# Attention and quantized feed-forward on one core: the gate's tokens prepared a step sooner, a piece per chunk, an earlier fetch, and idle products at the change of stages

## The chip, the core and the metric

The kernel runs on one core of a Trainium2 chip. A core has a matrix engine (TensorE, PE in the profile, with its weight loads in a row PEld of its own), a vector engine (VectorE, DVE), a scalar engine (ScalarE, ACT), a general engine (GpSimd, POOL) and a queue that issues transfers (SyncE, SP). Each engine takes its instructions in the order of the program. The metric is the device time of one execution in microseconds; of several executions the median is given.

## What is computed

The input `x` has 16 elements of 512 tokens of width 512. A cross attention with 16 heads over 120 context rows is added to it, then a feed-forward with gate and up weights (1536 x 512) and a down weight (512 x 1536). Both take a layer-normalized input:

```python
x = x + _L0_xattn_ref(_layernorm(x, axis=-1), ctx_1024, ctx_1024, Wq, Wk, Wv, Wo)
x = x + _L0_ffn_ref(_layernorm(x, axis=-1), w_gate, w_up, w_down)

def _L0_ffn_ref(x, w_gate, w_up, w_down):
    x = act_qdq(x)
    up = act_qdq(x @ lpbq_dequant(w_up).T)
    gate = act_qdq(x @ lpbq_dequant(w_gate).T)
    sig = fixed_qdq_u16(jax.nn.sigmoid(gate))
    gate = act_qdq(gate * sig)
    o = act_qdq(gate * up)
    return o @ lpbq_dequant(w_down).T
```

`act_qdq` rounds a whole tensor to 16-bit integers by a scale that comes from its largest absolute value. The scale of the feed-forward's input is therefore known only when the attention of all 16 elements is done, the gate's only when all gate products are done, and so on. That makes stages: attention, gate, up, down. `lpbq_dequant` rounds a weight to 4 bits in blocks of 32.

## The kernel before

**Attention** (lines up to 670) works through the 16 elements, transposes and quantizes the gate's weights on the way and leaves each element's output in `x1_d` in DRAM, with the mean and inverse deviation of each row in `ln_mv` and `ln_rstd`. Its last element ends with four output products (`output`, L416), row statistics, and a maximum of the normalized rows (`largest`). The first element of the feed-forward is held back transposed in the tiles `first`.

**The gate stage** (from line 674) first takes the largest value over all partitions (`over_all`: a product `line_x` at L694 and one `every_x` at L700) and from it the scale. Tokens are held as 16-bit integers (`xq`, one buffer). [...]each block of 128 features of an element is split into three *pieces*: the high part `hi` (`split_high`, L743), the low part `lo` (`split_low`, L746) and a mix `mix` of both (`split_mix`, L753). There are four blocks per element, and 8 buffers of each piece, that is two elements.

The work of an element is six chunks of two blocks of 128 gate outputs: 16 x 6 = 96 chunks, in order. `step(i)` is written so that TensorE runs ahead by half a chunk: `begin(i+1)` puts 8 products of the mixes into a new PSUM tile (L832; three tiles), ACT copies chunk i-1 out (L850, `t`, three buffers), `divide(i+1)` scales the new tile on ACT (L838), a `middle()` follows, then `rest(i)` adds 16 products of low and high pieces (L767), then an `after()`. In what follows, *step f of element b* is `step(6 b + f)`. `begin` of the first chunk of element b+1 stands at the head of step 5 of element b and is the first to read the pieces of b+1.

The preparation of element b+1 is spread over these hooks, by hand:

- `load` (L879, SP): `x1_d[b+2]` into the one buffer `x1t`, after step 2 of element b
- `normalize` (L883, POOL): four operations, after step 4
- `quantize` (L891, ACT, and L894, SP): a cast of the tile to 16-bit integers and a transposing transfer into `xq`, in the middle of step 0 of the next element (step 1 for element 1)
- `high`: four operations on POOL after steps 1 and 2 (for element 1: two on VectorE and two on POOL, after steps 3 and 4)
- `low` with the mix: two blocks after step 2, one after step 3, one after step 4 (for element 1: two after step 3, two after step 4)
- `keep` (L804, SP) stores `xq` for the up stage after step 2; `short_mixes` (L810, ACT) shortens the mixes and stores them too.

After each step VectorE also takes two maxima of chunk i-1 (`largest`, L855), and the dictionary `jobs` holds the preparation of the up weights (12 blocks, one per element from element 1 on) and of the down weights (4 blocks of three times the size, turned in elements 3, 6, 9, 12): load, quantize on VectorE (L142 to L152), turn on TensorE (L160), and the rest on VectorE, ACT and POOL (L169 to L172) with stores on SP. `when` gives the steps of the four jobs of an up weight.

The order on TensorE, VectorE, ACT and POOL in the gate stage is that of the program text (`manual_schedule`); SP's order is found by the compiler. The weights come through `Weights.load` (L738): 36 tiles of 256 KB on SP, 12 before the tokens of element 0, 24 after `load(1)`.

Of the kernel before, what the change touches and what calls it, by code (L numbers as in the profile page):

```python
# [9 lines left out]
F32 = mybir.dt.float32  # L10
# [11 lines left out]
P = 128  # L22
# [31 lines left out]
def tile_xattn_ffn(  # L54
# [32 lines left out]
    ident = const.tile([P, P], F32, name="ident")  # L87
# [12 lines left out]
    x1_d = [dram.tile([NQ, P, D], F32, name=f"x1_{b}") for b in range(B)]  # L100
# [22 lines left out]
    class WeightBlock:  # L123
# [7 lines left out]
        def load(self):  # L131
            self.wt = self.pool.tile(
                [P, self.I], F32, tag=f"raw_{self.tag}", name=f"wt_{self.nm}", bufs=1
            )
            nc.sync.dma_start(self.wt, self.w[ts(self.o, P), :])

        def quantize(self):
            pool, I, tag, nm = self.pool, self.I, self.tag, self.nm
            nb = I // WBLOCK
            wb = self.wt.rearrange("p (n k) -> p n k", k=WBLOCK)  # L140
            s = pool.tile([P, nb], F32, tag=f"s_{tag}", name=f"ws_{nm}", bufs=1)
            nc.vector.tensor_reduce(s, wb, AX.X, ALU.max, apply_absolute_value=True)  # L142
            nc.vector.tensor_scalar(s, s, 1.0 / 7.0, SCALE_MIN, ALU.mult, ALU.max)
            r = pool.tile([P, nb], F32, tag=f"r_{tag}", name=f"wr_{nm}", bufs=1)
            nc.vector.reciprocal(r, s)
            q = pool.tile([P, I], I16, tag=f"q_{tag}", name=f"wq_{nm}", bufs=1)
            qb = q.rearrange("p (n k) -> p n k", k=WBLOCK)
            nc.vector.tensor_tensor(
                qb, wb, r.unsqueeze(2).to_broadcast([P, nb, WBLOCK]), ALU.mult
            )  # L150
            nc.vector.tensor_scalar(q, q, 7.0, -8.0, ALU.min, ALU.max)
            nc.vector.tensor_tensor(  # L152
                wb, qb, s.unsqueeze(2).to_broadcast([P, nb, WBLOCK]), ALU.mult
            )
# [28 lines left out]
    with ExitStack() as at:  # L183
# [12 lines left out]
        def bank(nm):  # L196
            return ps_w.tile([P, 512], F32, tag="w", name=nm)
# [78 lines left out]
        class Element:  # L276
# [195 lines left out]
        ones = wpool.tile([P, P], F32R, name="ones")  # L472
# [34 lines left out]
        rep = wpool.tile([P, NG, P], F32R, name="rep")  # L507
# [161 lines left out]
        last.end_normalize(NQ - 1, nc.vector)  # L669
        last.largest(NQ - 1)  # L670

    H = S // 2
    N2 = NF // 2
    small = ctx.enter_context(tc.tile_pool(name="small", bufs=1))
# [6 lines left out]
    ones = small.tile([2, P], F32, name="ones")  # L681
# [91 lines left out]
    flat = lambda t: t.rearrange("p h f t -> p (h f t)")  # L773
    halves = lambda t: t.rearrange("p f (h t) -> p h f t", t=H)
    part = lambda t, b, f: t[b, :, :, 2 * f : 2 * f + 2, :]
# [5 lines left out]
    with ExitStack() as gu:  # L781
# [5 lines left out]
        class Tokens:  # L787


            def __init__(self, b, nm):  # L790
                self.b, self.nm, self.p = b, f"{nm}_{b}", []
                self.q = xpool.tile([P, NQ, ND, P], I16, tag="xq", name=f"xq_{self.nm}", bufs=1)

            def high(self, d, engine):
# [17 lines left out]
                    nc.sync.dma_start(xn_d[self.b], self.n)  # L812

            def fetch(self):
                nc.sync.dma_start(self.q, xq_d[self.b])
                self.n = xpool.tile([P, ND, S], I16, tag="xn", name=f"xn_{self.nm}", bufs=1)
                nc.sync.dma_start(self.n, xn_d[self.b])
# [4 lines left out]
        class Chunk:  # L822
# [25 lines left out]
            def out(self, dst):  # L848
                self.t = xpool.tile([P, 2, 2, H], F32, tag="t", name=f"t_{self.nm}", bufs=3)
                nc.scalar.copy(self.t, halves(self.ps))  # L850
# [8 lines left out]
        wp = wprep.__enter__()  # L859
        wg = Weights(wg_d, "wg")  # L860
        wu = Weights(wu_d, "wu")
        wd = Weights(wd_d, "wd")
        wg.load((0, 1), (0,))
        wg.load((0, 1), (1, 2))
        wg.load((2, 3))
        s_x, r_x = scale_of(over_all([max_x], "x"), 1.0, "x")
        s_xw = small.tile([P, 1], F32, name="s_xw")

        xs = {0: Tokens(0, "g")}
        for i, t in enumerate(first):  # L870
            nc.vector.tensor_scalar(
                xs[0].q[:, 2 * i : 2 * i + 2], t.rearrange("p q (d t) -> p q d t", t=P),
                r_x, None, ALU.mult,
            )

        def load(b):
            xs[b] = Tokens(b, "g")
            xs[b].x1 = wp.tile([P, NQ, D], F32, tag="x1t", name=f"x1t_{b}", bufs=1)
            nc.sync.dma_start(xs[b].x1, x1_d[b].rearrange("q p d -> p q d"))  # L879

        def normalize(b):
            for q in range(NQ):
                nc.gpsimd.tensor_scalar(  # L883
                    xs[b].x1[:, q, :], xs[b].x1[:, q, :],
                    ln_mv[:, b, q, 0:1], ln_rstd[:, b, q : q + 1], ALU.subtract, ALU.mult,
                )

        def quantize(b):

            xi = wp.tile([P, NQ * D], I16, tag="xi", name=f"xi_{b}")  # L890
            nc.scalar.activation(  # L891
                xi, xs[b].x1.rearrange("p q d -> p (q d)"), AF.Copy, scale=r_x
            )
            nc.sync.dma_start_transpose(xs[b].q.rearrange("p q d t -> p (q d) t"), xi)  # L894


# [22 lines left out]
        for d in range(ND):  # L919
            xs[0].high(d, nc.vector if d < 2 else nc.gpsimd)  # L920
            xs[0].low(d)
        xs[0].keep()
        load(1)
        normalize(1)
        wg.load(range(4, NF))
        nc.vector.tensor_scalar(s_xw, s_x, WHOLE, None, ALU.mult)

# [10 lines left out]
        def step(i, before=None, middle=None, after=None):  # L938
# [14 lines left out]
            if after:  # L953
                after()

        chunks[0].x = xs[0]
        chunks[0].begin()
        chunks[0].divide()
# [2 lines left out]
        jobs = {}  # L961
        for o in range(NF):
            start = (o + 1) * N2
            when = ((1, 2, 4, 5), (0, 1, 3, 4), (0, 1, 4, 5))[o % 3]
            for j, job in zip(when, up_weight(o)):
                jobs.setdefault(start + j, []).append(job)
        for o in range(ND):
            start = (3 * o + 2) * N2
            for j, job in zip((4, 5, 7, 8, 9, 10), down_weight(o)):
                jobs.setdefault(start + j, []).insert(0, job)  # L970
        for b in range(B):
            for f in range(N2):
                i = b * N2 + f

                def middle():
                    if f == (0 if b else 1) and b + 1 < B:
                        quantize(b + 1)
                    if f in (2, 3) and b < B - 2:
                        xs[b].short_mixes(wp, ((0, 1), (2, 3))[f - 2])

                def after():

                    if b == 0:
                        high = {3: ((0, nc.vector), (1, nc.gpsimd), (2, nc.gpsimd)), 4: ((3, nc.vector),)}
                        low = {3: (0, 1), 4: (2, 3)}
                    else:
                        high = {k: ((2 * k - 2, nc.gpsimd), (2 * k - 1, nc.gpsimd)) for k in (1, 2)}
                        low = {2: (0, 1), 3: (2,), 4: (3,)}
                    if b + 1 < B:
                        for d, engine in high.get(f, ()):  # L990
                            xs[b + 1].high(d, engine)
                        for d in low.get(f, ()):
                            xs[b + 1].low(d)
                    if i > 0:
                        chunks[i - 1].largest(max_g, **size)
                        chunks[i - 1].largest(top_g)
                    for job in jobs.pop(i, ()):
                        job()
                    if f == 2 and b + 1 < B - 2:
                        xs[b + 1].keep()  # L1000
                    if f == 2 and b + 2 < B:
                        load(b + 2)
                    if f == 4 and b + 2 < B:
                        normalize(b + 2)
                    if b == B - 1:
                        wu.load((0,) if f == 0 else (2 * f - 1, 2 * f))

                if b == B - 1 and f == 0:
                    wprep.__exit__(None, None, None)
                step(i, None, middle, after)  # L1010


# [80 lines left out]
        for k in range(NCH):  # L1093
            i, n = NCH + k, k // N2
            f = k % N2
# [43 lines left out]
            if k == 2:  # L1139
# [8 lines left out]
                low = small.tile([P, 1], F32, name="low")  # L1148
# [55 lines left out]
    with ExitStack() as dn:  # L1204
# [272 lines left out]
```

## Time and profile before

| | |
|---|---|
| three runs, median | 2636.52 us (2636.18 to 2639.85) |
| the profiled execution, whole | 2643.51 us |
| the profiled execution, its span | 2641.7 us, mean granted TensorE clock 0.977 |
| attention | to about 940 us |
| gate products | 946.66 to 1516.11 us |
| up products, then down products | the rest |

The slices of the page show where TensorE is not full:

```profile
PE   8899999999999779999999999999999399999999
...
PEclk9899999999999889999999999999999699999999
```

Each digit is a fortieth of the span, 66 us. Slices 14 and 15 are the change from attention to gate; the low digit at slice 32 is the change from up to down.

A line of the timeline reads: start, length, engine, line of the program, operation, tile written <- tiles read, partitions x elements, count; in brackets the idle time of the engine before it and what ended it.

### The profile page before, as it was taken

To read this page: it belongs to the slowest core of one execution; us is meant where nothing else is said; L and a number is where in the kernel's file an instruction comes from. 1 tells how busy PE (TensorE), PEld (TensorE's weight loads), DVE (VectorE), ACT (ScalarE), POOL (GpSimd) and SP (SyncE) were. 2 spreads that over 40 slices of the span, in tenths; PEclk is the share of its full clock that TensorE was granted. 3 is DMA by queue.
4 is the path that set the end of the run, shared out by engine and by line. 5 is a ranking of instruction groups with operands and counts; after the bars stand their busy time and mean duration, and the time that the engine had idled before them with its cause. 6 is when DMAs were issued, how large, how long until landed. Compare 5 with 4: busy or idle time off the path is not lost. (4 is left out here: it accounts for less than half of the span.)

```text
span 2641.7 us, 30187 instructions
## 1 busy us (share of the span) xinstructions
PE 2510.0 (95%) x10610; PEld 1674.0 (63%) x10610; DVE 2095.2 (79%) x2833; ACT 1155.9 (44%) x1311; POOL 1577.0 (60%) x1011
## 2 busy tenths in 40 slices
PE   8899999999999779999999999999999399999999
PEld 4334434334433258877877888888777278888887
DVE  4668877887797657787877579999998778888886
ACT  1222222222222224544444478887777244444442
POOL 4466665665765344645555147776765467777775
PEclk9899999999999889999999999999999699999999
DMA  4011121111120086757666789988988877777774
GB/s 159 20 64 48 68 87 48 52 56 61 55 72 17 32 278 214 242 189 237 218 211 207 238 298 331 325 308 290 315 301 308 299 277 250 250 250 251 251 253 144
DMA packets 268145, 500.48 MB, mean 189 GB/s; under 512 B 47440, under 2 KB 66000, under 8 KB 267984
## 3 DMA queue, kind: packets, MB, share of 16 engines
q1 hardware_dynamic: 267824, 497.94, 55.1%
q8 instruction: 84, 1.38, 0.2%
q14 instruction: 77, 0.63, 0.1%
q0 software_dynamic: 160, 0.52, 0.0%
HBM read 263.00 MB, written 227.54 MB: 186 GB/s over the span
## 5 line engine op out<-in xcount | busy, mean ns | idle before, releaser
L743 POOL TENSOR_SCALAR oh_d<-oq_d 128x512 fp32r<-128x512 int16 x190 | 398.9, 2122 | 154.3 <-DVE oq_d L1267 154.3
L1059 POOL TENSOR_TENSOR po<-gt,t_wu 128x1024 f32<-128x1024 f32 x96 | 231.7, 2413 | 204.0 <-DVE gt L1036 158.4
L309 PE MATMUL qp<-xnT,wq_sb 128*128 128x512 f32 x512 | 239.2, 610 | 2.6 <-ACT cT L205 2.6
L390 ACT COPY ao<-pv 128x512 f32<-128x512 f32 x64 | 37.5, 586 | 452.5 <-PE pv L381 452.5
L416 PE MATMUL op<-wo_sb,ao 128*128 128x512 f32 x512 | 233.2, 604 | 0.2 <-DVE ao L410 0.2
L832 PE MATMUL mm_wg<-xm_g,wg 128*128 128x512 f32 x768 | 200.1, 401 | 20.3 <-DVE xm_g L753 15.1
L1284 PE MATMUL dn_d<-wd,om_d 128*128 128x512 f32 x768 | 195.0, 404 | 17.5 <-DVE om_d L753 8.9
L767 PE MATMUL mm_wg<-xl_g,wg 128*128 128x512 f32 x768 | 210.2, 396 | 0.0
L767 PE MATMUL mm_wg<-xh_g,wg 128*128 128x512 f32 x768 | 208.8, 394 | 0.0
L855 DVE TENSOR_REDUCE max_g<-t_wg 128x1 f32<-128x1024 f32 x96 | 116.7, 1215 | 112.1 <-ACT t_wg L850 111.9
L743 POOL TENSOR_SCALAR xh_g<-xq_g 128x512 fp32r<-128x512 int16 x60 | 117.4, 1979 | 130.6 <-DMA xq_g<-xi 110.2
L1267 DVE SCALAR_TENSOR_TENSOR oq_d<-pq_d,r_o,uq_d 128x1024 int16<-128x1024 int16 x96 | 127.7, 1330 | 82.1 <-ACT uq_d L1220 82.1
L221 POOL TENSOR_TENSOR rt_q<-rt_q,sin_q 128x512 f32<-128x512 f32 x64 | 81.3, 1270 | 185.1 <-DVE rt_q L218 185.1
L1284 PE MATMUL dn_d<-wd,ol_d 128*128 128x512 f32 x768 | 184.7, 389 | 0.4 <-ACT dn_d L1296 0.4
L767 PE MATMUL mm_wu<-xl_u,wu 128*128 128x512 f32 x672 | 182.4, 393 | 2.6 <-ACT mm_wu L838 2.6
L1284 PE MATMUL dn_d<-wd,oh_d 128*128 128x512 f32 x768 | 184.5, 389 | 0.0
L1284 PEld LDWEIGHTS dn_d<-wd,om_d 128*128 128x128 f32 x768 | 145.0, 193 | 62.3 <-DVE om_d L753 19.3
L767 PE MATMUL mm_wu<-xh_u,wu 128*128 128x512 f32 x672 | 179.8, 389 | 0.0
L309 PEld LDWEIGHTS qp<-xnT,wq_sb 128*128 128x128 f32 x512 | 93.2, 192 | 135.1 <-issue 111.1
L832 PEld LDWEIGHTS mm_wg<-xm_g,wg 128*128 128x128 f32 x768 | 143.4, 191 | 55.1 <-DVE xm_g L753 21.4
L336 DVE TRANSPOSE_TENSOR_REDUCE mt<-st 128x32 f32<-128x1024 f32 x128 | 151.7, 1223 | 30.2 <-PE st L330 29.9
L832 PE MATMUL mm_wu<-xm_u,wu 128*128 128x512 f32 x672 | 168.3, 393 | 1.5 <-ACT t_wu L850 1.1
(255 smaller groups left out, 5584.5 us busy)
## 6 DMA issues: line engine op xcount, KB each, us to landing
g_d<-t_wg SPq DMA_DIRECT2D x96, 512.0 KB, 3.7
gt<-g_d SPq DMA_DIRECT2D x96, 512.0 KB, 5.1
u_d<-t_wu SPq DMA_DIRECT2D x96, 512.0 KB, 6.0
p_d<-gt SPq DMA_DIRECT2D x96, 512.0 KB, 5.3
p<-p_d SPq DMA_DIRECT2D x96, 512.0 KB, 4.8
u<-u_d SPq DMA_DIRECT2D x96, 512.0 KB, 5.7
xt<-in_x_dram SPq DMA_DIRECT2D x16, 1024.0 KB, 5.4
x<-xt SPq DMA_DIRECT2D x16, 1024.0 KB, 4.3
```

Of the source, the lines that this page charges most:

```text
L221: nc.gpsimd.tensor_tensor(v(t), v(t), sin, ALU.mult)
L309: nc.tensor.matmul(ps, lhsT=wq_sb[:, d, ts(g, P)], rhs=self.xnT[:, d, :], start=(d == 0), stop=(d == ND - 1),)
L336: nc.vector.tensor_reduce(self.mt[:, 2 * i : 2 * i + 2, 0, :], self.st[i].rearrange("p h (c j) -> p h c j", j=DK), AX.X, ALU.max, apply_tr ...
L390: nc.scalar.copy(self.ao[:, g, :], pv)
L416: nc.tensor.matmul(ps, lhsT=self.ao[:, g, ts(q, P)], rhs=wo_sb[:, g, :], start=(g == 0), stop=(g == NG - 1),)
L743: engine.tensor_scalar(as_runs(p.hi, q), q, TO_256, TO_256, ALU.add, ALU.subtract)
L767: nc.tensor.matmul(ps[:, j, :], lhsT=lhs(j, i)[k], rhs=rhs(j, i)[k], start=(k == 0 and i == 0), stop=(k != 1 and i == n - 1), skip_group_c ...
L832: nc.tensor.matmul(self.ps[:, j, :], lhsT=lhs(j, d), rhs=self.x.p[d].mix, start=(d == 0), stop=(d == ND - 1), skip_group_check=True,)
L855: nc.vector.tensor_reduce(maxes[:, i : i + 1], self.t, AX.XYZ, ALU.max, **how)
L1059: nc.gpsimd.tensor_tensor(flat(g.po), flat(g.tile), flat(c.t), ALU.mult)
L1267: nc.vector.scalar_tensor_tensor(out=oq.rearrange("p f t -> p (f t)"), in0=pq, scalar=r_o, in1=uq, op0=ALU.mult, op1=ALU.mult,)
L1284: nc.tensor.matmul(self.ps[j], lhsT=self.p[f // 2].all()[k][:, f % 2, ts(j, P)], rhs=wd.made[f][k], start=(k == 0 and f == 0), stop=(k != ...
```

## The change

1. `idle_0`: 18 products of `ones` and `rep` with 512 columns after the last work of the attention, into a PSUM tile that nobody reads. `idle_1`: 14 products of `ident` with itself, 128 columns, in front of the first gate products.
2. Element 1 of the gate stage is fetched between the weight loads, and normalized in front of `keep` of element 0. The buffer `xq` is now taken in `room()`, when it is written, and not when the `Tokens` object is made.
3. From element 2 on everything is put forward: `load` from step 2 to step 0 of element b (element 0: stays at 2), `normalize` from step 4 to two halves after steps 2 and 3 (element 0: 3 and 4), `quantize(b + 2)` to the middle of step 5 of element b, `keep` from step 2 to step 1.
4. The high pieces come after steps 0 and 1, the low ones one per step after steps 1 to 4. For element 1: high after steps 2 and 3, low after 2, 3 (two) and 4.
5. Up weights 0, 3, 6, 9 take steps 0, 1, 3, 4 in place of 1, 2, 4, 5.

```diff
+        idle = bank("idle_0")
+        for _ in range(18):
+            nc.tensor.matmul(
+                idle, lhsT=ones, rhs=rep.rearrange("p g m -> p (g m)"), start=True, stop=True
+            )
...
+
+            def room(self):
                 self.q = xpool.tile([P, NQ, ND, P], I16, tag="xq", name=f"xq_{self.nm}", bufs=1)
...
-        wg.load((0, 1), (0,))
-        wg.load((0, 1), (1, 2))
-        wg.load((2, 3))
+        xs = {0: Tokens(0, "g")}
...
+        wg.load((0, 1))
+        wg.load((2, 3), (0,))
+        load(1)
+        wg.load((2, 3), (1, 2))
...
+            xs[b].room()
             nc.sync.dma_start_transpose(xs[b].q.rearrange("p q d t -> p (q d) t"), xi)
...
+        normalize(1, range(NQ))
         xs[0].keep()
-        load(1)
-        normalize(1)
         wg.load(range(4, NF))
...
+        idle = bank("idle_1")
+        for _ in range(14):
+            nc.tensor.matmul(idle[:, :P], lhsT=ident, rhs=ident, start=True, stop=True)
...
-            when = ((1, 2, 4, 5), (0, 1, 3, 4), (0, 1, 4, 5))[o % 3]
+            when = ((0, 1, 3, 4), (0, 1, 3, 4), (0, 1, 4, 5))[o % 3]
...
-                    if f == (0 if b else 1) and b + 1 < B:
-                        quantize(b + 1)
+                    if b == 0 and f == 1:
+                        quantize(1)
+                    if f == 5 and b + 2 < B:
+                        quantize(b + 2)
...
                     if b == 0:
-                        high = {3: ((0, nc.vector), (1, nc.gpsimd), (2, nc.gpsimd)), 4: ((3, nc.vector),)}
-                        low = {3: (0, 1), 4: (2, 3)}
+                        high = {2: ((0, nc.vector), (1, nc.gpsimd), (2, nc.gpsimd)), 3: ((3, nc.vector),)}
+                        low = {2: (0,), 3: (1, 2), 4: (3,)}
                     else:
-                        high = {k: ((2 * k - 2, nc.gpsimd), (2 * k - 1, nc.gpsimd)) for k in (1, 2)}
-                        low = {2: (0, 1), 3: (2,), 4: (3,)}
+                        high = {k: ((2 * k, nc.gpsimd), (2 * k + 1, nc.gpsimd)) for k in (0, 1)}
+                        low = {k + 1: (k,) for k in range(ND)}
...
-                    if f == 2 and b + 1 < B - 2:
+                    if f == (1 if b else 2) and b + 1 < B - 2:
                         xs[b + 1].keep()
-                    if f == 2 and b + 2 < B:
-                        load(b + 2)
-                    if f == 4 and b + 2 < B:
-                        normalize(b + 2)
+                    if b + 2 < B:
+                        if f == (0 if b else 2):
+                            load(b + 2)
+                        if f in ((2, 3) if b else (3, 4)):
+                            normalize(b + 2, (0, 1) if f == (2 if b else 3) else (2, 3))
```

`load` moves in front of the weight loads without a change in its body; in `normalize` the loop runs over the rows `qs` that it is given.

More of the change, by code (lines that the diff above doesn't have):

```diff
@@ L814, in fetch @@
             def fetch(self):
+                self.room()
                 nc.sync.dma_start(self.q, xq_d[self.b])
@@ L862, in tile_xattn_ffn, with load @@
         wd = Weights(wd_d, "wd")
-        wg.load((0, 1), (0,))
-        wg.load((0, 1), (1, 2))
-        wg.load((2, 3))
+        xs = {0: Tokens(0, "g")}
+        def load(b):
+            xs[b] = Tokens(b, "g")
+            xs[b].x1 = wp.tile([P, NQ, D], F32, tag="x1t", name=f"x1t_{b}", bufs=1)
+            nc.sync.dma_start(xs[b].x1, x1_d[b].rearrange("q p d -> p q d"))
+        wg.load((0, 1))
+        wg.load((2, 3), (0,))
+        load(1)
+        wg.load((2, 3), (1, 2))
         s_x, r_x = scale_of(over_all([max_x], "x"), 1.0, "x")
         s_xw = small.tile([P, 1], F32, name="s_xw")
-        xs = {0: Tokens(0, "g")}
+        xs[0].room()
         for i, t in enumerate(first):
@@ L874, in tile_xattn_ffn, with normalize @@
             )
[L876 to L882, printed above, removed]
+        def normalize(b, qs):
+            for q in qs:
                 nc.gpsimd.tensor_scalar(
```

## The prediction

> **What bounds the kernel now.** I read the page's totals and slices first, then the groups, then the stage that the diff touches: waits by stretch, a table of stretches, the timeline.
>
> ```profile
> span 2641.7 us, 30187 instructions
> PE 2510.0 (95%) x10610; PEld 1674.0 (63%) x10610; DVE 2095.2 (79%) x2833; ACT 1155.9 (44%) x1311; POOL 1577.0 (60%) x1011
> ...
> L832 PE MATMUL mm_wg<-xm_g,wg 128*128 128x512 f32 x768 | 200.1, 401 | 20.3 <-DVE xm_g L753 15.1
> ```
>
> TensorE is busy 95% of the span, so only its gaps can be won. The page's chain of waits is no guide here: its shares add up to some 18% and name lines of the last stage (oh_d, ol_d). The group row is: in the gate stage TensorE waits 15.1 us for VectorE's mixed piece `xm_g`, the first operand of each new element.
>
> How much is lost in that stage? It runs from 946.66 us (first gate product) to 1516.11 us (last): 569.4 us. Undisturbed, a step starts 5.44 us after the last one (24 products, four in 0.907 us in the timeline) and a weight turn adds 0.46. 96 steps, the next stage's first 8 products (1.81) and 24 turns make 535.4. So 34 us are lost, and the timeline places them, each as the time from one undisturbed start to the next less the ideal: stage start 5.7; first products of element 1: 6.6 (981.36 to 993.44, less 5.44); of element 5: 6.0; 8: 5.8; 11: 7.6; 14: 2.2. The other elements start without a gap. The loss at 5:
>
> ```profile
> 1106.28 3.01 SPq L894 DMA_TRANSPOSE xq_g<-xi  x1
> ...
> 1110.82 7.61 POOL L743 TENSOR_SCALAR xh_g<-xq_g 128x512 fp32r<-128x512 int16 x4 [7.83 <-PE mm_wg L767]
> ...
> 1118.67 0.68 DVE L142 TENSOR_REDUCE ws_wu<-wt_wu 128x16 f32<-128x512 f32 x1
> ...
> 1122.04 0.68 DVE L746 TENSOR_TENSOR xl_g<-xq_g,xh_g 128x512 fp32r<-128x512 int16 x1
> 1122.18 0.66 PE L160 MATMUL tp_wu<-ident,wt_wu 128*128 128x128 f32 x4 [0.51 <-DVE wt_wu L152]
> ...
> 1123.83 1.21 DVE L855 TENSOR_REDUCE max_g<-t_wg 128x1 f32<-128x1024 f32 x1
> ...
> 1126.09 0.67 DVE L746 TENSOR_TENSOR xl_g<-xq_g,xh_g 128x512 fp32r<-128x512 int16 x1
> ...
> 1127.54 0.73 PE L832 MATMUL mm_wg<-xm_g,wg 128*128 128x512 f32 x2 [2.85 <-DVE xm_g L753]
> ```
>
> The transpose of element 5's tokens lands at 1110.8, 12 us before they are needed; from then VectorE works without a pause: two pieces, the maxima of a chunk, the quantizing of an up weight (3.4 us from 1118.67), a third piece, maxima, the fourth piece. TensorE waits for the third and the fourth (0.19, 2.85) and for the weight (0.51). After it products take twice as long: the table of stretches gives clock 0.95 over 1110 to 1142, 0.90 at element 11, 1.00 where the longest gap was 1.91 (element 14).
>
> **Elements 5, 8, 11, 14.** All four parts of the preparation go forward: normalizing from step 4 of element b-2 to steps 2 and 3 (element 0: 3 and 4), ACT's cast and the transpose from step 0 of b-1 to step 5 of b-2, the high halves (POOL) from steps 1, 2 to 0, 1, the lower pieces from 2, 2, 3, 4 to 1, 2, 3, 4. In elements 1, 4, 7, 10 the up weight also goes from steps 1, 2, 4, 5 to 0, 1, 3, 4. No operation is added. I follow VectorE from S, the start of step 5 (TensorE's last products of chunk 4 are done): ACT copies (1.0) and divides (1.0, after 1.81 of new products), then casts 2.0: S+5.1. Transpose issued, landing 4.5 later as in the rows of elements 2 to 6: S+9.7. POOL's first high half 1.9: S+11.7. VectorE: piece (1.09+0.69), maxima (2.35), weight (3.2): 7.3; two steps of piece and maxima, 4.1 each; the last piece 1.8: S+29.1. Needed by S+34.5 (5.44+27.7+1.4). So 5 us to spare where there were minus 3: the stalls with their slow clock go: **-6.0 -5.8 -7.6 -2.2 = -21.5 us**.
>
> **What is late next: the elements with a down weight** (3, 6, 9, 12). There VectorE also has 7.4 us of quantizing in step 5 of the element before and 1.4 a step for turned blocks. Before, its streak from 1162.36 to 1187.33 ends in such a block; ACT scales it (0.63) ahead of the copy (1.0) that frees the PSUM tile TensorE wants next: copy done 1188.90, tile used at 1189.55; less the usual 0.25 from engine to engine, 0.4 to spare. The same work stands in the streak afterwards (a piece moves from step 2 to 1, both inside), but TensorE will no longer have lost 6 us at element 5: before, VectorE idled 2.26 us ahead of the streak, a cover that then is gone. ACT's copy also waits behind the scale of the up weight's block of the step before. Bounds: 0 each if VectorE has caught up, 2.3 each (that idle time) if not; I take 1 each at three of them: **+3**. A gain is excluded: the streak keeps its length.
>
> **Element 1.**
>
> ```profile
> 948.56 19.53 SPq L738 DMA_DIRECT2D wg<-wg_d  x24
> ...
> 968.50 0.63 SPq L851 DMA_DIRECT2D g_d<-t_wg  x1
> 969.24 5.01 SPq L894 DMA_TRANSPOSE xq_g<-xi  x1
> ...
> 976.26 0.43 DVE L743 TENSOR_SCALAR xh_g<-xq_g 128x512 fp32r<-128x512 int16 x1 [5.48 <-DMA xq_g<-xi]
> ...
> 986.49 1.22 PE L832 MATMUL mm_wg<-xm_g,wg 128*128 128x512 f32 x2 [1.05 <-DVE xm_g L753]
> ```
>
> Its fetch goes in front of four weight loads: POOL normalizes from about 952.5 (issue 3.3 us sooner, and 948.6 when its own queue is free) instead of 957.20, and ACT casts at 962.6 instead of 965.50, its place in ACT's queue. But SP issues in order, and the 24 weight loads hold it to 968.1, at the rate of the transfers (6 MB in 19.5 us); bytes and order there stay. So the transpose is still issued at 969.24 and lands at 976.2. What then comes: VectorE's first piece now stands at step 2, *ahead* of a chunk's maxima, which before were done at 968.4 while nothing else could run. They move behind the wait: first piece 978.4, maxima 980.8, VectorE's own high half 981.2, second piece 982.9, third 984.3, maxima 986.7, fourth 988.3, against 986.44 before: **+2**. Bounds: if SP's order (nobody writes it out) puts the transpose where the cast is done (964.6), all is 4.6 sooner and the slow clock (3.3 of the 6.6) may go: -5; +3 with a longer gap. I take +2, by the row of the loads.
>
> **Start of the stage: the idle products.** 18 products of 512 columns behind the last attention product, by the gate products' spacing 18 x 0.227 = 4.1 us, from 934.83 to 938.9; the next thing TensorE does waits for VectorE until 940.46, which covers them by 1.5. 14 of 128 columns follow `every_x` (done 942.0). Such a product is not in the trace; nearest are the turns (0.115 each, 1.6 us) and, above, a 512-column f32 product (0.43 each, 6.0 us, done 948.0). The first gate product waits for VectorE's piece until 946.66: cost 0, at most 1.4. What they buy: the first 16 gate products ran at half clock (14 took 6.87 us), because TensorE had been idle since 934.8. The Trainium skill (TensorE: Matmul & The Clock Gate, Part 1) says that a window of about 3.4 us of idleness halves the clock and activity keeps it whole; here a gap of 2.84 us (from 911.35) was already followed by a clock of 0.50, so the gaps left by the pieces (1.3 us each with two products between) may still break it. By the rule the saving is 16 x (0.43-0.227) = 3.2 us. By the trace it is next to nothing, since the weights are late next:
>
> ```profile
> 959.70 1.88 PE L832 MATMUL mm_wg<-xm_g,wg 128*128 128x512 f32 x7 [0.38 <-DMA wg<-wg_d]
> ```
>
> Chunk 2 had its second weight only at 959.70, after the same bytes as afterwards. A faster start waits there. I take **-0.4**; 0 and -3.2 are the ends.
>
> **SP.** Transposes, stores of blocks and chunks share one queue. Before, a transpose left 0.03 us after its cast, and 2.5 late at elements 5, 8, 11 behind a weight load. I allow **+1** in all.
>
> **Sum.** -21.5 +3 +2 -0.4 +1 = -15.9. TensorE has no gap to speak of from 1516 to 1900 (299.70 of 300 us busy from 1600), so it reaches the end. The profiled execution took 2643.5 (span 2641.7); it would take 2627.6. The shown median is 2636.5, 7 lower; the difference carried over gives **2620.6 us**.
>
> **The rivals.**
> - *Late transposes (slower).* VectorE takes its work in order, and the first lower piece at step 1 now stands ahead of maxima and weight. In a down-weight element VectorE gets to it at S+13.5 and its high half is there at S+11.7: 1.8 us of slack. If SP holds the transpose back by L behind stores that wait for VectorE (SP waited 41.5 us for `wt_wu` over the stage, 9.7 at longest), four elements lose L-1.8 each, and 3.3 more for the clock once the gap is over 2.8. It decides from L of about 5; at 8 it is 4 x 9.5 = 38 in place of 3 and +19 in all: 2655. For it: order on SP is free. Against: at step 5 those stores are mostly done. 13%.
> - *Everything goes.* The transpose of element 1 finds a place before the weights and the down elements keep up: -21.5 -5 -0.4, about -27: 2610. Against: the 24 loads were ready first before. 15%.
> - *Given back.* VectorE (79% busy, and busy without pause over 25 us) is the next bound: down elements lose 2.3 each at all four, transposes 2 late, and part of the stalls at 5, 8, 11 stays (a third, 7): -21.5+7+9.2+2+2 = about -1: 2635. 14%.
> - *My sum*, -9 to -22: 58%.
>
> **Numbers.** A change under 0.2% (5.3 us) can't be told from none. Faster by more: the sum, "everything" and the upper edge of "given back", 0.76; within 0.2%: 0.11; slower: 0.13. Range: from "everything" with its bound (2608) to just over the time before (2639), which leaves out the late transposes.
>
> **What would show it.** Right: no wait for `xm_g` at elements 5, 8, 11, 14 and clock 1.00 there; at element 1 a wait at least as long; a DMA wait or a short gap in front of chunk 2's products however the first ones run; small gaps in elements 6, 9, 12. Wrong: transposes that land more than 12 us after step 5 begins; gate-stage VectorE waiting for POOL's `xh_g` with TensorE idle behind it; the transpose of element 1 issued before the weights are through.

## The result, and the profile after

The changed kernel takes 2629.09 us, the median of 7 runs (2624.07 to 2629.57). The kernel before takes 2636.52 us, the median of 7 runs beside it (2635.06 to 2641.85). The ratio is 0.9961, with a 95% interval of 0.995 to 0.9973: some 10 us less, where the interval reaches from 7 to 13. The forecast was faster, by 15.9 us, at 2620.6 us. The direction is right, and the time lies in the range but 8.5 us above the point.

First the page of the changed kernel: span, totals, the slices of TensorE, and the group of the gate's mix products.

```profile
span 2622.3 us, 30272 instructions
...
PE 2500.4 (95%) x10656; PEld 1676.1 (64%) x10656; DVE 2087.5 (80%) x2833; ACT 1155.5 (44%) x1311; POOL 1574.3 (60%) x1011
...
PE   8899999999999889999999999999999399999999
...
L841 PE MATMUL mm_wg<-xm_g,wg 128*128 128x512 f32 x768 | 197.7, 398 | 11.6 <-DVE xm_g L759 8.7
```

VectorE's instructions are as many as before (2833), so nothing got cheaper there; the idle time in front of the mix products fell from 20.3 to 11.6 us, and what waits for VectorE's pieces from 15.1 to 8.7. Slices 14 and 15 went from 7 to 8. The lines have moved: begin is L841 (was L832), the low and high products L773 (L767), the copy L859 (L850), the pieces L749, L752 and L759 (L743, L746, L753), the transpose L907 (L894).

Next the waits of TensorE in the gate stage of the changed kernel, without those among the first 16 products (total in us, times, longest):

```profile
PE mm_wg L841 <- DVE xm_g L759: 7.1, 5, 2.6
PE mm_wg L841 <- ACT t_wg L859: 2.5, 4, 0.8
PE mm_wg L841 <- DMA wg<-wg_d: 0.3, 1, 0.3
```

The middle row is new. It is ACT's copy that frees a PSUM tile; no such wait stood among the losses before.

The gate stage, from the first gate product to the last, took 569.45 us before and 554.72 after: 14.7 us less. The spans differ by 19.4. The other 4.7 lie outside the stage, where the change adds no more than 18 idle products, and the experiments show below that this part moves by up to 10 us from one execution to the next. So I read every kernel by the length of its gate stage and by its waits, and its total by the ratio.

Losses by place, measured as in the prediction (time from one undisturbed start to the next, less the ideal 5.44 us of each step between them and 0.46 where a weight turn falls in between):

| place | before | forecast change | after | change |
|---|---|---|---|---|
| start of the stage | 5.7 | -0.4 | 4.9 | -0.8 |
| element 1 | 6.6 | +2 | 7.1 | +0.5 |
| elements 5, 8, 11, 14 | 21.5 | -21.5 | 0.5, 2.8, 2.7, 0 | -15.5 |
| down-weight elements | 0 | +3 | 1.0 | +1.0 |
| late transposes | 0 | +1 | none of its own | 0 |
| sum | 33.8 of 34 | -15.9 | 19.0 of 19.3 | -14.8 |

That is the stage's 14.7 us but for 0.1. One profile is one execution: in the second profiles of both kernels (below) the start loses 5.8 and 5.2, element 1 loses 5.4 and 7.8, the four elements 20.6 and 5.9.

The table of stretches for the changed kernel, at element 5, where a clock of 0.95 had stood (columns: stretch, its length, busy time and instructions of PE, PEld, DVE, ACT, POOL, granted clock, DMA share, GB/s):

```profile
1110.00:1142.00 32.00, 31.84 (x143) 26.05 (x142) 24.79 (x30) 15.42 (x18) 15.82 (x9) 1.00 0.67 216
```

TensorE is idle for 0.16 of 32 us and the clock is whole. Half of the stall is left at element 8, and a third at 11. Element 8 in the timeline of the changed kernel:

```profile
1194.78 5.19 SPq L907 DMA_TRANSPOSE xq_g<-xi  x1
...
1203.66 7.61 POOL L749 TENSOR_SCALAR xh_g<-xq_g 128x512 fp32r<-128x512 int16 x4 [5.88 <-DMA xq_g<-xi]
...
1205.63 1.09 DVE L752 TENSOR_TENSOR xl_g<-xq_g,xh_g 128x512 fp32r<-128x512 int16 x1 [5.99 <-POOL xh_g L749]
...
1210.87 0.69 DVE L142 TENSOR_REDUCE ws_wu<-wt_wu 128x16 f32<-128x512 f32 x1 [1.17 <-DMA wt_wu<-in_L_ffn_w_up_dram]
...
1222.13 0.68 DVE L752 TENSOR_TENSOR xl_g<-xq_g,xh_g 128x512 fp32r<-128x512 int16 x1
...
1223.59 0.73 PE L841 MATMUL mm_wg<-xm_g,wg 128*128 128x512 f32 x2 [1.38 <-DVE xm_g L759]
...
1227.21 0.63 ACT L171 ACTIVATE wt_wu<-wt_wu 128x512 f32<-128x512 f32 x1 [8.88 <-DVE wt_wu L170]
...
1228.79 2.14 PE L841 MATMUL mm_wg<-xm_g,wg 128*128 128x512 f32 x8 [0.80 <-ACT t_wg L859]
```

Step 5 of element 6 begins at S = 1187.46. The tokens land at S+16.2, where the prediction had S+9.7. VectorE then stands idle for 6 us in front of the first piece, waits another 1.17 for the up weight that now is due a step sooner, and has the fourth piece ready at S+36.1; TensorE wanted it at S+34.8. Then VectorE comes late to the turned weight, ACT holds its scale (L171) in front of the copy, and the PSUM tile is 0.80 late. The loss is of the same kind as before, 2.8 us in place of 5.8. Two of the signs that the prediction had named for being wrong stand in these rows: a transpose that lands more than 12 us after step 5 begins, and VectorE waiting for POOL's `xh_g` with TensorE idle behind it.

### The profile page after: what moved, and what is told of

Same layout as the page of the kernel before. It is cut to its first block, busy times and chain, and to the rows that moved or that the text cites. A ratio compares the mean times of both kernels' runs of the same rounds, so it can differ in the third digit from the quotient of the medians.

```text
span 2622.3 us, 30272 instructions
## 1 busy us (share of the span) xinstructions
PE 2500.4 (95%) x10656; PEld 1676.1 (64%) x10656; DVE 2087.5 (80%) x2833; ACT 1155.5 (44%) x1311; POOL 1574.3 (60%) x1011
## 5 line engine op out<-in xcount | busy, mean ns | idle before, releaser
L749 POOL TENSOR_SCALAR oh_d<-oq_d 128x512 fp32r<-128x512 int16 x190 | 398.9, 2122 | 153.2 <-DVE oq_d L1286 153.2
L841 PE MATMUL mm_wg<-xm_g,wg 128*128 128x512 f32 x768 | 197.7, 398 | 11.6 <-DVE xm_g L759 8.7
L773 PE MATMUL mm_wg<-xl_g,wg 128*128 128x512 f32 x768 | 206.3, 391 | 0.0
L773 PE MATMUL mm_wg<-xh_g,wg 128*128 128x512 f32 x768 | 205.8, 390 | 0.0
L749 POOL TENSOR_SCALAR xh_g<-xq_g 128x512 fp32r<-128x512 int16 x60 | 117.2, 1978 | 122.3 <-DMA xq_g<-xi 116.8
L773 PE MATMUL mm_wu<-xl_u,wu 128*128 128x512 f32 x672 | 180.7, 391 | 1.4 <-ACT mm_wu L847 1.4
L773 PE MATMUL mm_wu<-xh_u,wu 128*128 128x512 f32 x672 | 179.7, 389 | 0.0
L841 PEld LDWEIGHTS mm_wg<-xm_g,wg 128*128 128x128 f32 x768 | 142.5, 190 | 45.7 <-DVE xm_g L759 12.6
L841 PE MATMUL mm_wu<-xm_u,wu 128*128 128x512 f32 x672 | 166.8, 390 | 4.5 <-ACT t_wu L859 4.5
```

Of the source, the lines that this page charges most:

```text
L749: engine.tensor_scalar(as_runs(p.hi, q), q, TO_256, TO_256, ALU.add, ALU.subtract)
L773: nc.tensor.matmul(ps[:, j, :], lhsT=lhs(j, i)[k], rhs=rhs(j, i)[k], start=(k == 0 and i == 0), stop=(k != 1 and i == n - 1), skip_group_c ...
L841: nc.tensor.matmul(self.ps[:, j, :], lhsT=lhs(j, d), rhs=self.x.p[d].mix, start=(d == 0), stop=(d == ND - 1), skip_group_check=True,)
```

## The experiments

Stage is the length of the gate stage in the profiled execution, outside is its span less that, both in us. Ratios are to the kernel before on the same chip, with their 95% intervals.

| run | what it is | ratio | stage | outside |
|---|---|---|---|---|
| before_again | the kernel before, one execution | | 567.62 | 2073.7 |
| after_again | the change | 0.9947 (0.9928 to 0.9965) | 555.79 | 2077.1 |
| no_idle | change without idle products | 0.9939 (0.9921 to 0.9958) | 552.91 | 2071.1 |
| idle_only | before with idle products | 0.9998 (0.9985 to 1.0011) | 566.71 | 2072.5 |
| steady_only | parts 3, 4 (from element 2), 5 alone | 0.994 (0.992 to 0.9959) | 553.72 | 2069.2 |
| when_only | part 5 alone, on before | 0.9998 (0.9988 to 1.0009) | 568.40 | 2069.1 |
| when_old | change without part 5 | 0.9946 (0.9931 to 0.996) | 549.53 | 2074.9 |
| late_t | change with the transpose at its old step | 1.0055 (1.0041 to 1.0069) | 577.18 | 2072.0 |
| el1_order | change, element 1 in another order | 0.9967 (0.9952 to 0.9981) | 554.17 | 2076.3 |
| t_first | change, element 1's transpose before the last weights | 0.9975 (0.9965 to 0.9985) | 557.64 | 2073.5 |
| best | when_old and el1_order without idle products | 0.9898 (0.9883 to 0.9913) | 542.57 | 2072.8 |

### The two kernels once more

> The kernel before once more, for its profile. Theory: gate stage 566 to 571 us as in the first profile and in idle_only, with the rest of the span anywhere from 2067 to 2078 us; so the 19 us between the first two profiles were the stage's 14.7 and 5 us of chance outside it. Rival: the stage itself is 560 us or less here.

> The changed kernel once more, for a second profile. The first two profiles differ by 19.4 us of span, the medians by 7.4 only. If the gate stage is what changed, its length from the first gate product to the last is 554 to 556 us here too (it was 554.7, before 569.4) and the rest of the span varies from run to run by some 5 us. If the first profile was a lucky one in the gate stage, that stage is 559 to 563 us here. Ratio to the kernel before 0.995 to 0.997.

The stages repeat within 2 us (569.45 and 567.62; 554.72 and 555.79), a gain of 13.3 between the means. The rest of the span went from 2067.6 to 2077.1 for the same changed kernel. That is twice the 5 us that was expected. A difference of 5 us in one span says nothing here, one of 5 us in the stage does. By the ratio this comparison gives 14 us less (9 to 19), an interval that overlaps the first one.

### The idle products

No_idle drops both loops from the change, idle_only puts both into the kernel before:

```diff
-        idle = bank("idle_0")
-        for _ in range(18):
...
-        idle = bank("idle_1")
-        for _ in range(14):
...
```

> The changed kernel without both groups of idle products. By the step that took their worth as 0.4 us: first gate products at half clock again, but chunk 2 waits for its weights all the same, the stage is at most 0.5 us longer and the ratio is that of the changed kernel to within 0.0005. Rival, the rule of the clock gate in full: 3.2 us longer, ratio higher by 0.0012.

> The kernel before with both groups of idle products and nothing else. Mine: the clock stays whole over the first gate products, and the third chunk's products begin within 0.5 us of the time before, counted from the end of the attention; ratio 0.9995 to 1.0005. Rival (the clock gate gives 3.2 us): ratio 0.9988.

Neither ratio shows a gain or a loss: idle_only is at 1 within 0.15%, and no_idle lies inside the interval of after_again. In the traces the idle products do something. In the changed kernel's first profile (the 14 products of `idle_1` are counted as 28 rows):

```profile
932.30 4.69 PE L674 MATMUL idle<-rep,ones 128*128 128x512 f32 x18
...
939.67 5.02 PE L970 MATMUL idle<-ident 128*128 128x128 f32 x28
944.45 0.85 PE L841 MATMUL mm_wg<-xm_g,wg 128*128 128x512 f32 x2
...
947.65 4.88 PE L841 MATMUL mm_wg<-xm_g,wg 128*128 128x512 f32 x12 [0.60 <-DVE xm_g L759]
...
956.73 1.88 PE L841 MATMUL mm_wg<-xm_g,wg 128*128 128x512 f32 x7 [0.34 <-DMA wg<-wg_d]
```

And in the second profile of the same program:

```profile
941.83 3.39 PE L970 MATMUL idle<-ident 128*128 128x128 f32 x28
946.55 0.84 PE L841 MATMUL mm_wg<-xm_g,wg 128*128 128x512 f32 x2 [1.33 <-DMA wg<-wg_d]
948.47 6.78 PE L841 MATMUL mm_wg<-xm_g,wg 128*128 128x512 f32 x14 [1.09 <-DVE xm_g L759]
```

In the first, the idle products themselves run slowly (5.02 us; the table of stretches gives clock 0.73 and then 0.54 under them), and the gate products after them speed up sooner. In the second the idle products run at full clock (3.39 us, 1.00), and the gate products that follow are slow (6.78 for 14, clock 0.54). In no_idle, without them, the 14 products took 7.30 us. Here is the whole slow stretch after the attention, in the table of stretches of the kernel before:

```profile
937.74:954.81 17.07, 8.15 (x17) 4.88 (x18) 10.74 (x22) 1.01 (x1) 4.80 (x6) 0.50 0.87 304
```

and of the change, in its first profile:

```profile
940.89:944.30 3.41, 3.41 (x18) 3.41 (x17) 3.31 (x6) 0.00 (x0) 2.00 (x2) 0.50 0.93 288
944.30:947.71 3.41, 1.80 (x9) 0.86 (x7) 3.31 (x6) 0.00 (x0) 2.03 (x1) 1.00 1.04 368
947.71:951.13 3.42, 3.28 (x7) 2.17 (x8) 1.24 (x3) 0.84 (x1) 0.92 (x1) 0.50 1.05 392
```

So the idle products don't keep the clock whole, but they shorten the time at half clock: it is 17.1 us in all six traces without them, 6.8 in six of the seven with them and 3.4 in the last (late_t). In the first profile more than half of what is saved lies in front of the first gate product, where TensorE has little to do. Counted from the last product of the attention, the fourth chunk begins at 29.3 us in idle_only, where the kernel before has 30.2 and 30.3, and at 29.2 and 29.4 with the change, where no_idle has 30.4: some 1 us is gained, a third of the 3.2 us that the rival of idle_only asked for. (Its third chunk was expected within 0.5 us of the time before; it begins 1.0 and 1.8 us sooner than in the two profiles.) Chunk 2 is then met by the weight that is not there yet (0.34 in the change, 0.41 in idle_only), as forecast. The rest of the gain doesn't reach the end: no_idle was expected to be up to 0.5 us longer, but its stage is 1.8 and 2.9 us shorter than in the two profiles of the change. By place, elements 1, 5, 8, 9 and 11 lose less there.

### The steady part, and the up weights' steps

Steady_only keeps only what holds from element 2 on, with element 1 and its fetch as before and no idle products. When_old takes part 5 out of the change, and when_only puts that one part into the kernel before:

```diff
-            when = ((0, 1, 3, 4), (0, 1, 3, 4), (0, 1, 4, 5))[o % 3]
+            when = ((1, 2, 4, 5), (0, 1, 3, 4), (0, 1, 4, 5))[o % 3]
```

> Of the change only what concerns elements 2 to 15 (fetch, normalizing, cast, pieces, weight steps); element 1 prepared and fetched as before, no idle products. By the step that puts the gain at elements 5, 8, 11 and 14: all of the gain and no loss of 0.5 to 2 us at element 1, so as fast as the changed kernel or up to 2 us faster. Rival, the start of the stage gives a good part: 3 us or more slower than the changed kernel.

> The changed kernel with the up weights 0, 3, 6, 9 at their old steps 1, 2, 4, 5. Theory (what removes the waits is the earlier transpose and one piece per step; VectorE has time to spare with either steps): no wait of 2 us for a mix at elements 5, 8, 11, gate stage 551 to 556 us. Rival (moving the weight is what removes them): waits of 2 to 3 us come back at elements 5, 8 and 11 and the stage is 562 us or more.

> The kernel before, with the up weights 0, 3, 6, 9 at steps 0, 1, 3, 4 and nothing else. Theory: there the pieces still come late, so the waits at elements 5, 8 and 11 shrink by little (the quantizing no longer stands between the third and the fourth piece, but VectorE is as full), stage 563 to 572 us, ratio 0.998 to 1.002. Rival: this part alone takes the waits away: stage below 560 us.

Steady_only has the whole gain (0.994, stage 553.72), as expected. The early fetch of element 1 and the idle products add nothing to it; element 1 loses 5.2 us there, in place of 7.1 and 7.8.

Part 5 is worth less than nothing beside the others. Without it there is no wait left at elements 5, 8 and 11, and the stage is 5.2 us shorter. The waits of TensorE in the gate stage of when_old:

```profile
PE mm_wg L841 <- DVE xm_g L759: 4.8, 3, 2.4
```

The 4.8 are all at element 1; the row for ACT's copy is gone. By place, elements 5, 8 and 11 lose nothing (6.0 us with the change) and the down-weight elements nothing (1.0), while element 1 loses 9.0 in place of 7.1. At element 8 step 5 of element 6 begins at 1188.81 there. The cast is done 5.1 us later, as the prediction had it, against 7.3 in the changed kernel, where ACT's scale of a down-weight block, due from VectorE, is in front of it. The tokens land at S+11.8, the fourth piece is ready at S+30.2, and it is needed at S+33.1.

Alone, on the kernel before, part 5 does take most of the waits for pieces away, and gives as much back. The waits of when_only:

```profile
PE mm_wg L832 <- ACT t_wg L850: 6.0, 9, 0.8
PE mm_wg L832 <- DVE xm_g L753: 5.5, 5, 2.1
PE tp_wd L160 <- DVE wt_wd L170: 5.2, 3, 1.8
```

Behind the first 16 products, pieces cost 5.5 in place of 14.3, where little change had been expected; but the down weights' turns and ACT's copy now cost 11.2. The stage is 568.40 and the ratio 0.9998. The pieces' early start does the same work without that price, and where it is made, the new steps only crowd VectorE in front of the pieces (at element 8 the weight's quantizing stands before the second piece, and in when_old before the third). How much of it comes from the earlier transpose (part 3) and how much from one piece per step (part 4) is not shown: no run has one of them alone, with everything else as before. In total time when_old can't be told from the change (0.9946 and 0.9947); that it is better rests on the stage and on the waits.

### The late transpose

> The changed kernel with cast and transpose of elements 2 to 15 back at step 0 of the element before them (one step of 5.44 us later), everything else as changed: the pieces at their new places. Theory of the late transposes (VectorE takes its work in order, slack 1.8 us in elements with a down weight, 5 us in the others): 3.6 us lost in each of elements 3, 6, 9, 12, with a slow clock behind some of them, stage 568 to 582 us, that is as slow as before the change or slower. Rival (slack is larger than worked out): stage below 562 us.

```diff
-                    if f == 5 and b + 2 < B:
-                        quantize(b + 2)
+                    if f == 0 and b > 0 and b + 1 < B:
+                        quantize(b + 1)
```

Cast and transpose start a step later while VectorE's pieces keep their new, early place. The kernel is now slower than before by 0.55%, and the stage is 22.5 us longer than with the change. The two waits of TensorE that are the longest in sum, and VectorE's wait at the first piece:

```profile
PE mm_wg L841 <- DVE xm_g L759: 14.5, 10, 2.4
PE mm_wg L841 <- ACT t_wg L859: 6.9, 11, 0.8
...
DVE xl_g L752 <- POOL xh_g L749: 83.1, 14, 10.1
```

With the change that last line reads:

```profile
DVE xl_g L752 <- POOL xh_g L749: 40.8, 10, 6.0
```

This is the rival of the late transposes, made to happen: VectorE stands at the first piece with maxima and weights queued behind it, and all of them get late. Its mechanism is real; the change stays clear of it by less than 5.44 us. The stage came as expected, but not by the expected sum, which had 3.6 us at each of elements 3, 6, 9 and 12 and next to nothing at 5, 8 and 11. By place, elements 3, 6, 9 and 12 lose 7.2, 2.4, 2.6 and 2.3, and 5, 8 and 11 lose 4.0, 4.7 and 4.1.

### Element 1

Two ways to be rid of its stall. El1_order puts the maxima of chunk 1 in front of the first piece, and the fourth piece in front of the maxima of chunk 2:

```diff
-                        low = {2: (0,), 3: (1, 2), 4: (3,)}
+                        low = {2: (0,), 3: (1, 2, 3)}
...
+                    if i == 2:
+                        chunks[1].largest(max_g, **size)
+                        chunks[1].largest(top_g)
...
-                    if i > 0:
+                    if i > 0 and i != 2:
```

> The changed kernel, but for element 1 the maxima of chunk 1 stand ahead of its first pieces again, and its fourth piece ahead of the maxima of chunk 2. Theory (VectorE's order behind the wait for the transpose makes the loss at element 1, which is 7.1 and 7.8 us in the two profiles of the changed kernel): all four mixes done about 980.5 when the first is needed at 978.4 and the fourth at 979.8, loss 1 to 2 us, gate stage 549 to 551 us (changed kernel 554.7 and 555.8). Rival (the transpose itself lands too late whatever the order): loss above 4 us, stage 553 or more.

T_first loads the last weights behind element 1's transpose:

```diff
-        wg.load(range(4, NF))
+        wg.load(range(4, 10))
...
                         quantize(1)
+                        wg.load(range(10, NF))
```

> The changed kernel, with the last 6 of the 24 weight tiles loaded behind element 1's transpose. Theory (the weight loads on SP hold the transpose back, 966.28 where its cast is done at 961.56): the transpose is issued within 1 us of its cast, lands some 4.5 us sooner, the loss at element 1 falls from 7.1 to 0.5 to 3 us, gate stage 549 to 551 us. Rival (the bandwidth, not the queue: the transfer lands no sooner, or the last weights come late for chunk 5): no shorter than 554 us, with a wait for a weight.

In the changed kernel element 1 lost 7.1 us, in this order on the timeline:

```profile
966.28 5.34 SPq L907 DMA_TRANSPOSE xq_g<-xi  x1
...
973.58 0.43 DVE L749 TENSOR_SCALAR xh_g<-xq_g 128x512 fp32r<-128x512 int16 x1 [13.86 <-DMA xq_g<-xi]
...
985.08 1.22 PE L841 MATMUL mm_wg<-xm_g,wg 128*128 128x512 f32 x2 [2.64 <-DVE xm_g L759]
```

ACT's cast was done at 961.57; the transpose left 4.7 us later, behind the last of the weight loads. VectorE was idle for 13.86 us at the first piece with a chunk's maxima queued behind it.

El1_order leaves one wait of 0.93 at element 1, and the loss there falls from 7.1 to 1.6 us, as expected. But its stage is only 0.6 us shorter than that of the change, where 4 to 6 had been expected. By place, the 5.5 us are given back at elements 3 and 5, which lose 3.0 and 3.2 in place of 0 and 0.5. At these two there are new waits for pieces and for ACT's copy (0.77 at 1056.32 and 0.84 at 1080.86; 1.47 and 0.79 at 1123 and 1128). The reading that fits is that TensorE arrives sooner, and finds VectorE and ACT not as far ahead. The start loses 0.5 more, where the weight that chunk 2 waits for comes 0.78 late.

In t_first the transpose leaves 0.8 us after its cast (964.64 and 965.42) in place of 4.7, which is 2.8 us sooner counted from the first gate product, and its tokens land 1.6 us sooner. The waits of element 1 fall from 4.4 to 1.6 us, 0.48 of it for a weight, and the stage is 557.64, so the expectation failed. The fetch of element 2 now sits with the loads behind the transpose. In the timeline of t_first:

```profile
986.35 8.27 POOL L895 TENSOR_SCALAR x1t<-x1t,ln_mv,ln_rstd 128x512 f32<-128x512 f32 x4 [8.32 <-DMA x1t<-x]
...
994.66 2.00 ACT L903 ACTIVATE xi<-x1t,inv_x 128x2048 int16<-128x2048 f32 x1 [7.86 <-POOL x1t L895]
...
997.61 2.86 PE L841 MATMUL mm_wg<-xm_g,wg 128*128 128x512 f32 x8 [2.81 <-ACT t_wg L859]
```

POOL waits for the tile, ACT for POOL with the copy queued behind the cast, and TensorE for the copy. A stall was moved from the fetch of element 1 to the fetch of element 2.

### Both, without the tight places

> The changed kernel without idle products, with the up weights 0, 3, 6, 9 at their old steps, and with element 1's maxima and pieces in the order of el1_order. Theory: with the weights at their old steps the loss taken out at element 1 is no longer given back at elements 2, 3 and 5, so the stage is 543 to 547 us, 8 to 12 less than with the whole change and 4 to 6 less than when_old; ratio to before 0.991 to 0.994. Rival: VectorE is full whatever the order, the gain at element 1 is given back at an element with a down weight, stage 549 us or more.

Best takes the change without idle products, with the up weights at their old steps, and with el1_order's order. It is faster than both kernels: 2615.05 us, the median of 4 runs (2612.93 to 2617.20) beside 2641.64 for the kernel before. Its waits in the gate stage:

```profile
PE mm_wg L836 <- DMA wg<-wg_d: 4.9, 2, 4.6
PE mm_wg L836 <- DVE xm_g L754: 1.7, 2, 0.9
```

The 4.6 is in front of the first gate product, so it is no part of the stage's length (before it was 4.64). After one of 0.93 at 987.78 there is none until the stage's end. The same order that gave 0.6 us in el1_order gives 7.0 against when_old once part 5 is away: a gain in front counts only if what follows has room. By place the 7.0 are element 1 alone, with 1.7 us in place of 9.0; the start loses 5.4 in place of 5.0, so leaving out the idle products won nothing there. Of the 9.0 some may be chance: the change itself has 7.1 and 7.8, and the ten traces with neither this order nor t_first's loads lie between 5.2 and 9.0. The two with the new order have 1.6 and 1.7.

## Why the prediction was right, and where it was not

**Elements 5, 8, 11, 14: right in kind, mis-sized.** The stalls went at 14 and all but 0.5 us at 5, and the clock was whole at all four, but 15.5 us were won in place of 21.5. The 6.0 us that stayed are what the rival "given back" had for these elements ("a third, 7"). The term that failed is the transpose, "landing 4.5 later as in the rows of elements 2 to 6", and with it the "5 us to spare". At elements 5, 8 and 11 it took 7.6, 8.9 and 8.0 us from issue to landing, where the same three elements had 4.5 to 4.7 before. A step sooner it comes right behind the stores of down-weight blocks and the load of the next (at element 8 that load is issued at 1194.12, the transpose at 1194.78), and the DMA share while it is under way is 1.04 to 1.07 (0.84 to 0.94 before). In when_old it takes 6.3 to 6.7, at a share as high (1.06 to 1.10). A high share alone is not the cause: before, the transposes of elements 6 and 9 took 4.3 and 4.5 us at 1.01, and with the change that of element 7 took 5.1 us at 1.07. What makes the three slow stays open; no run isolates it. The rest is the cast, 2.2 us late at element 8 and 2.4 at 11 behind the down-weight block's scale (on time at 5), and the wait of 1.17 for the up weight; when_old has neither. The tokens so land at S+12.7, 16.2 and 15.5 at the three, in place of S+9.7. I had counted part 5 among what goes forward, "no operation is added", and not asked what it puts in front of the pieces.

**Down-weight elements.** The forecast was +3; one gap of 0.68 us (at 1286.18) and a loss of 1.0 came. That VectorE and ACT can be late there is seen in when_only (11.2 us of waits, half of them at the turns of down weights); with the pieces moved too there was nearly room enough. The slack of 1.8 us was set too low: element 9's tokens land at S+17.3 with the change, and TensorE waits for none of its pieces.

**Element 1.** The reasons held: the loads keep the transpose back (issued 4.7 us after its cast), and the maxima move behind the wait. The gap is "at least as long" (2.64 in place of 2.29). The loss is +0.5 in the first profiles and +2.4 in the second, in place of +2, with the transpose 0.8 us sooner in the first, counted from the start of the stage. The half clock is no consequence of the gap of 2.64: it begins at 981.85, and the gap at 982.44. The better end, -5, can't be had by moving the loads alone: t_first pays with the fetch of element 2.

**Start.** Forecast 0 for cost and -0.4 for gain. The loss fell by 0.8 in the first profiles and 0.6 in the second, the first gate product came 0.2 to 0.3 us sooner after the attention, and the ratio of idle_only shows nothing. Of rule and row, neither was right, and the row was nearer: the rule in the Trainium skill (TensorE: Matmul & The Clock Gate, Part 1) would have given 3.2 us. But no 3.4 us of idleness were needed to lose the clock: in the stretch 944.30 to 947.71 shown above TensorE was at work for 1.80 of 3.41 us at clock 1.00, and the next stretch has 0.50. The same part also says that the window runs freely, so that one kernel counts a different number of slow products from run to run; the two profiles of the change agree with that, and it was the sentence to weigh. The waiting weight came as forecast (0.34).

**Late transposes.** SP held none of the transposes of elements 5, 8 and 11 back (issued within 0.03 us of their casts); what came late is inside elements 8 and 11, so the allowance of +1 has no line of its own. The rival, at 13%, did not happen, though two of its signs came at element 8, and late_t shows that 5.44 us more would have brought it about.

**From the sum to the time.** The sum of -15.9 is near the measured -14.7 and -13.3, in part by luck: the first term was 6.0 us too high, and those of element 1, the down weights, the start and the transposes together 4.9 too low in gain. What missed by more is the time. To carry the 7 us over is to take the sum from the median before (2636.5 - 15.9), and with the stage's 14.7 in its place that would be 2621.8. The median fell by 7.4 only, and by the two ratios 7 to 13 and 9 to 19 us. The part outside the stage moves by up to 9.5 us between two executions of the changed kernel, and which part of the program it is stays open. That the forecast for the profiled execution (2627.6) lies 1.5 us from the median is chance: it starts from an execution 7 us above the median before.

## What to carry to other kernels

A step that is moved forward takes its transfers into another stretch: the landing time of the old place can't be carried along (4.5 us became 7.6 to 8.9 here), so allow for more, and ask what will stand in front of the step on each engine. In a hand-written order a stall that is removed early only counts if the engines behind it have room, so take out the tight places downstream (here a weight's job a step too soon) before judging the part upstream. When the total moves by as much from run to run as the change does, measure the stage and its waits.

## What the runs showed of the hardware that was not expected

Products that nobody reads shortened the time at half clock at the change of stages from 17.1 to 6.8 us and did not end it, and where the rest fell differed between two executions of one program: once under the idle products (28 rows in 5.02 us) and the gate products after them, once under the gate products alone (14 in 6.78 us).

The clock went by stretches and not by single gaps. In each of the 13 traces every change of the granted clock lies on a grid of 3.413 us. TensorE's idle time in each stretch of that grid, from 880 to 1530 us, can be added up (an estimate, as the ends of products are modelled). A whole clock was halved after a stretch with 1.48 us of idleness or more, never after less and always from 1.93 us on; half clock ended only after a stretch with 0.53 us or less. In the attention before 880 us stretches with 0.94 us were enough, so idle time is not the whole rule.

And a transposing transfer of the same size took 4.5 us in one place and 8.9 us, a step sooner, in another; the DMA share, 0.84 and 1.04, does not explain it by itself.
